# Slot projections: group sums taken by TensorE, and the inverse root spread by a product

## The chip, the cores and the metric

The kernel runs on one core of a Trainium2 chip. The time is device time in microseconds (us), from start to end of one execution. TensorE (PE; its weight loads PEld), VectorE (DVE), ScalarE (ACT) and GpSimd (POOL) each work through a queue of their own; SyncE (SP) issues most DMAs. The profile counts times from the first instruction of one profiled execution.

## The reference, cut to what matters

The input is an image of 512 x 512 positions with 64 channels. Two layers follow each other; the part that concerns us is the beginning of the first.

```python
x = x + _L0_conv_ref(_gn(x), ...)     # the first layer
...
def _ln(x, w, b):
    mu = jnp.mean(x, axis=-1, keepdims=True)
    var = jnp.var(x, axis=-1, keepdims=True)
    return (x - mu) * jax.lax.rsqrt(var + EPS) * w + b
xn = _ln(x, norm_w, norm_b)
left = xn @ left_w + left_b
right = xn @ right_w + right_b
m = sequence_mask.astype(xn.dtype)
mask = (m[:, :, None] * m[:, None, :])[..., None]
left = left * mask
right = right * mask
left = left * jax.nn.sigmoid(xn @ lgate_w + lgate_b)
right = right * jax.nn.sigmoid(xn @ rgate_w + rgate_b)
...
out = jnp.einsum('bkjd,bkid->bijd', left, right)
```

So each position is normalised over its 64 channels, projected to a left and a right side, and each side is multiplied by a gate. Where the mask is zero, left and right are zero; the kernel therefore computes them only for the rows and columns that the mask keeps, the "slots".

## The kernel before

The kernel ranks the positions that the mask keeps. If no more than K = 256 are kept, which holds here, the function `compact` does the work. Its first stage reads the image, takes the statistics for the group norm, and copies the kept columns into one large buffer `xc` in SBUF: 128 partitions (kept rows, in two halves `r`), K + 1 columns, two halves, 64 channels. The second stage, which the change touches, makes the left and right sides from `xc` and stores them to DRAM (`left_d`, `right_d`). Later stages multiply the two sides (`tri_c_ps`), normalise, project, gate, add to the image and do the second layer.

The second stage works on 64 groups `q` of four kept columns each. A group is a tile of 128 x 512 elements. In "channel-major" form its partitions are 64 channels of row half 0 and 64 channels of row half 1, and its 512 elements are four columns by 128 rows. Each group passes through these functions:

- `channels(q)` (L704): four transposes by TensorE (L707) turn four columns of `xc` to channel-major form in PSUM (`xc_ps`); ScalarE applies the group norm's scale and offset (L709) and writes a tile `gc_t` in SBUF.
- `centered(q)` (L713): four matmuls (L716) with the tile as the stationary operand and the constant matrix `center` as the moving one. They subtract the mean over the channels, and turn the tile back: the result `cc_ps` has positions as partitions. ScalarE squares it (L720, `sqc`).
- in the loop, VectorE sums the squares over 64 channels (L778): eight sums for each partition and group (`total`). After four groups (QB = 4) there is a 128 x 32 tile.
- `factors(k)` (L726): nine small VectorE operations (L199 to L209, in `rsqrt_steps`) compute the inverse square root of the 128 x 32 tile. They are kept in a list `todo`, and each iteration of the loop issues the next three.
- `spread(q)` (L730): GpSimd copies the eight factors of a group to 64 channels each (L733, `rbc`, 128 x 512).
- `normed(q)` (L735): four transposes (L739) bring the factors to channel-major form in PSUM (`rc_ps`); VectorE multiplies `gc_t` by them (L741, `xnc`).
- `project(q, k)` (L743): matmuls with 64 rows (L747), one for each row half, for the gates and for the sides, into PSUM tiles of two banks each (`gates_c`, `sides_c`).
- ScalarE takes the sigmoid of the gates (L756, `sigc`); VectorE adds the bias to the sides and multiplies by the sigmoid (L773, two operations, `o_c`); SP issues two stores (L783).

The order is written out by hand: the engines take the operations in the order of the program. A loop runs over `q` from -10 to 63. One iteration issues, in this order: gates and sigmoid of group q; `normed(q + 1)`; up to three root steps; `spread(q + 2)`; `channels(q + 10)`; `centered(q + 9)`; sides and `o_c` of group q; the sums of squares of q + 9; the stores of group q. So ten iterations run ahead before the first gates, and the last ten have nothing left to centre. [...]PSUM banks of 2 KB are in use: two for `xc_ps`, one each for `cc_ps` and `rc_ps`, four for `gates_c` and `sides_c`, which have one buffer each. `sigc` has one buffer too.

A float32 matmul appears in the profile as two instructions, a transpose as one.

Of the kernel before, what the change touches and what calls it, by code (L numbers as in the profile page):

```python
# [9 lines left out]
F32 = mybir.dt.float32  # L10
I32 = mybir.dt.int32
AF = mybir.ActivationFunctionType
ALU = mybir.AluOpType
AX = mybir.AxisListType
PSUM = bass.MemoryType.PSUM
DRAM = bass.MemoryType.DRAM

P = 128
N = 512
C = 64  # L20
# [8 lines left out]
EPS = 1e-5  # L29
# [5 lines left out]
QB = 4  # L35
# [11 lines left out]
def conv_preact_kernel(ctx: ExitStack, tc: tile.TileContext, t: dict):  # L47
    nc = tc.nc
    x, out = t["x"], t["out"]
# [17 lines left out]
    ident = load_const("c_ident", [P, P])  # L67
    center = load_const("c_center", [P, P])
# [13 lines left out]
    with tc.tile_pool(name="ix", bufs=1) as xp, tc.tile_pool(  # L82
        name="ixp", bufs=1, space=PSUM
# [105 lines left out]
            step()  # L189
        return out  # L190

    def rsqrt_steps(pool, total, scale, eps, shape, y=None):

        v, w, h, out = (pool.tile(shape, F32, name="rq_" + k) for k in ("v", "w", "h", "out"))
        if y is None:
            y = pool.tile(shape, F32, name="rq_y")
        vec = nc.vector
        return out, [
            lambda: vec.tensor_scalar(v, total, scale, eps, ALU.mult, ALU.add),  # L199
            lambda: vec.tensor_scalar(y.bitcast(I32), v.bitcast(I32), -0.5, float(0x5F3759DF), ALU.mult, ALU.add),  # L200

            lambda: vec.tensor_mul(w, y, v),
            lambda: vec.tensor_mul(h, w, y),
            lambda: vec.scalar_tensor_tensor(h, h, -10.0 / 3.0, h, ALU.add, ALU.mult),
            lambda: vec.scalar_tensor_tensor(y, h, 5.0, y, ALU.add, ALU.mult),

            lambda: vec.tensor_mul(w, y, v),
            lambda: vec.scalar_tensor_tensor(w, w, -0.5 * 27.0 / 512.0, y, ALU.mult, ALU.mult),
            lambda: vec.scalar_tensor_tensor(out, w, 9.0 / 16.0, y, ALU.add, ALU.mult),  # L209
        ]  # L210
# [402 lines left out]
    def compact(fc):  # L613
# [31 lines left out]
        with tc.tile_pool(name="xc", bufs=1) as cp:  # L645
            xc = cp.tile([P, K + 1, 2, C], F32, name="xc")
            with tc.tile_pool(name="f1", bufs=1) as sp, tc.tile_pool(name="f1x", bufs=2) as xp, tc.tile_pool(
                name="f1y", bufs=4
# [19 lines left out]
                for jc in range(NJ):  # L668
                    if jc % quarter == 0:
                        stats = sp.tile([P, 1, 16 * quarter, 6], F32, name="stats1c")  # L670
                    for r in range(4):
                        flat = xgs[jc][1][r].rearrange("p j c -> p (j c)")
# [18 lines left out]
                ab1 = group_norm_affine(fc, sets, 2 * stats.shape[2], "xc")  # L691


            with tc.tile_pool(name="fb", bufs=QB + 8) as gp, tc.tile_pool(name="fw", bufs=2) as wk, tc.tile_pool(
                name="fr", bufs=3
            ) as rp, tc.tile_pool(name="fg", bufs=1) as sp, tc.tile_pool(name="fo", bufs=2) as op, tc.tile_pool(
                name="fpt", bufs=2, space=PSUM
            ) as pt, tc.tile_pool(name="fpc", bufs=1, space=PSUM) as pc, tc.tile_pool(
                name="fpp", bufs=1, space=PSUM
            ) as pp, tc.manual_schedule():  # L700
                groups = K // 4
                gts, totals, rss, rbs, xns, todo = {}, {}, {}, {}, {}, []

                def channels(q):  # L704
                    tps = pt.tile([P, 4, P], F32, name="xc_ps")
                    for i in range(4):
                        nc.tensor.transpose(tps[:, i, :], xc[:, 4 * q + i].rearrange("p r c -> p (r c)"), ident)  # L707
                    gts[q] = gp.tile([P, N], F32, name="gc_t")
                    nc.scalar.activation(  # L709
                        gts[q], tps.rearrange("p i k -> p (i k)"), AF.Identity, bias=ab1[:, 1:2], scale=ab1[:, 0:1]  # L710
                    )

                def centered(q):  # L713
                    cps = pc.tile([P, 8, C], F32, name="cc_ps")
                    for i in range(4):
                        nc.tensor.matmul(  # L716
                            cps[:, 2 * i : 2 * i + 2, :], gts[q][:, i * P : (i + 1) * P], center, start=True, stop=True
                        )
                    sq = wk.tile([P, 8, C], F32, name="sqc")
                    nc.scalar.activation(sq, cps, AF.Square)  # L720
                    k, n = divmod(q, QB)
                    if n == 0:
                        totals[k] = rp.tile([P, QB * 8], F32, name="total")
                    return sq, totals[k][:, 8 * n : 8 * n + 8]

                def factors(k):  # L726
                    rss[k], steps = rsqrt_steps(rp, totals.pop(k), 1.0 / C, EPS, [P, QB * 8])
                    todo.extend(steps)

                def spread(q):  # L730
                    k, n = divmod(q, QB)
                    rbs[q] = rp.tile([P, 8, C], F32, name="rbc")
                    nc.gpsimd.tensor_copy(rbs[q], rss[k][:, 8 * n : 8 * n + 8].unsqueeze(2).to_broadcast([P, 8, C]))  # L733

                def normed(q):  # L735
                    rps = pc.tile([P, N], F32, name="rc_ps")
                    flat = rbs.pop(q).rearrange("p (i r) c -> p i (r c)", r=2)
                    for i in range(4):
                        nc.tensor.transpose(rps[:, i * P : (i + 1) * P], flat[:, i, :], ident)  # L739
                    xns[q] = wk.tile([P, N], F32, name="xnc")  # L740
                    nc.vector.tensor_mul(xns[q], gts.pop(q), rps)  # L741

                def project(q, k):  # L743
                    ps = pp.tile([P, 2, N], F32, name=k + "_c")
                    for r in range(2):
                        h = slice(r * C, (r + 1) * C)
                        nc.tensor.matmul(ps[:, r, :], weights[k][h], xns[q][h], start=True, stop=True)  # L747
                    return ps


                for q in range(-QB - 6, groups):
                    live = lambda i: 0 <= q + i < groups
                    if live(0):
                        gates = project(q, "gates")
                        sig = sp.tile([P, 2, N], F32, name="sigc")
                        nc.scalar.activation(sig, gates, AF.Sigmoid, bias=biases["gates"])  # L756
                    if live(1):
                        normed(q + 1)
                    for step in todo[:3]:
                        step()  # L760
                    del todo[:3]
                    if live(2):
                        spread(q + 2)
                    if live(QB + 6):
                        channels(q + QB + 6)
                    if live(QB + 5):
                        sq, total = centered(q + QB + 5)
                    if live(0):
                        sides = project(q, "sides")
                        xns.pop(q)  # L770
                        res = op.tile([P, 4, 2, P], F32, name="o_c")
                        for r in range(2):
                            nc.vector.scalar_tensor_tensor(  # L773
                                res[:, :, r, :], sides[:, r].rearrange("p (i k) -> p i k", i=4), biases["sides"],
                                sig[:, r].rearrange("p (i k) -> p i k", i=4), ALU.add, ALU.mult,
                            )
                    if live(QB + 5):
                        nc.vector.tensor_reduce(total, sq, AX.X, ALU.add)  # L778
                        if (q + QB + 5) % QB == QB - 1:
                            factors((q + QB + 5) // QB)  # L780
                    if live(0):
                        for side, dst in enumerate((left_d, right_d)):
                            nc.sync.dma_start(  # L783
                                dst[:, 4 * q : 4 * q + 4, :].rearrange("c j k -> c (j k)"),
                                res[side * C : (side + 1) * C].rearrange("c j r k -> c (j r k)"),
                            )
# [20 lines left out]
        with tc.tile_pool(name="tri", bufs=1) as trp:  # L807
# [17 lines left out]
            with tc.tile_pool(name="ti", bufs=4) as ip, tc.tile_pool(name="tt", bufs=3) as tp, tc.tile_pool(  # L825
                name="tpt", bufs=4, space=PSUM
            ) as ps_t, tc.tile_pool(name="tpo", bufs=3, space=PSUM) as ps_o:
                for c in range(C):
                    sides = []
                    for name, src in (("left", left_d), ("right", right_d)):  # L830
                        raw = ip.tile([P, 2, K], F32, name=name + "_raw")
                        nc.sync.dma_start(raw, src[c].rearrange("(b p) k -> p b k", p=P))
                        tps = ps_t.tile([P, 2, K], F32, name="side_ps")
# [31 lines left out]
            with tc.manual_schedule(), tc.tile_pool(name="late", bufs=1) as lp:  # L865
# [65 lines left out]
                with tc.tile_pool(name="np_x", bufs=LEAD + 2) as tp, tc.tile_pool(  # L931
                    name="np_y", bufs=2
                ) as yp, tc.tile_pool(name="np_q", bufs=2) as sqp, tc.tile_pool(
                    name="np_s", bufs=3
                ) as small, tc.tile_pool(name="oz", bufs=4) as zp, tc.tile_pool(
                    name="o1", bufs=1
# [15 lines left out]
                    totals = [scratch[:, i, : SIZE * 8] for i in range(2)]  # L952

                    factors = [scratch[:, i, SIZE * 8 :] for i in range(2)]
                    eps = lp.tile([P, 1], F32, name="eps")
# [420 lines left out]
def _constants():  # L1376
# [19 lines left out]
    for part, rows_ in enumerate(((c.T, -s.T), (s.T, c.T))):  # L1396
# [6 lines left out]
        "c_last_mask": last_mask,  # L1403
        "c_pick4": (np.arange(P) % 32 % MODES % 4)[:, None] == np.arange(4)[None, :],
        "c_col_inv": col_inv.reshape(P, 2, 4, P),
        "c_turn": np.kron([[0, 1], [-1, 0]], np.eye(C)),
        "c_iota": np.tile(np.arange(N), (P, 1)),
        "c_tri": np.triu(np.ones((P, P))),
# [33 lines left out]
```

## Time and profile before

| | |
|---|---|
| median of three runs | 1838.84 us (1837.78 to 1840.75) |
| profiled execution | 1839.54 us, its span 1837.7 us |
| mean granted TensorE clock | 0.894 |
| slot projections | from about 206 to 466 us of the span |
| stores of the sides | 64 of 256 KB for each side |

Operations of the stage, each with its count and median duration in ns:

| operation | engine | count | ns |
|---|---|---|---|
| `gc_t`, 128x512 from PSUM | ACT | 64 | 770 |
| `sqc`, 128x512 from PSUM | ACT | 64 | 595 |
| `sigc`, 128x1024 from PSUM | ACT | 64 | 1114 |
| `total`, 128x512 to 128x8 | DVE | 64 | 677 |
| root steps, 128x32 | DVE | 9 x 16 | 174 to 193 |
| `xnc`, 128x512 | DVE | 64 | 679 |
| `o_c`, 128x512 | DVE | 128 | 746 |
| `rbc`, 128x512 | POOL | 64 | 613 |

How to read what follows: the timeline lists start, duration, engine, line, operation and tile, with a count where like instructions are merged. A matmul's duration runs until its end, and the next one starts before that, so the cost of a piece of TensorE's work is read from start to start. The list of waits gives the total in us, the times, and the longest.

### The profile page before, as it was taken

Reading aid. Unit: us, or ns where it says so; the run is one execution under the profiler, and the core shown is the slowest. Engines: PE = TensorE matmul, PEld = TensorE weight load, DVE = VectorE, ACT = ScalarE, POOL = GpSimd, SP = SyncE. Lnnn points to the kernel's source line nnn. Section 1 sums busy time; section 2 is a strip of 40 time slices with the busy share of each in tenths; the row PEclk is TensorE's granted clock in tenths of the full one; section 3 lists DMA queues with packets and bytes.
Section 4 is the critical chain, followed back from the end, with each engine's and each line's share of the span. In section 5 each row is a group of like instructions: output and inputs, shape, how many; then the busy total and the mean of one; then the engine's idle time right before and its main releaser. Section 6 shows DMA issues by size and latency. Waiting matters only on the chain.

```text
span 1837.7 us, 33577 instructions
## 1 busy us (share of the span) xinstructions
PE 1637.7 (89%) x11414; PEld 1287.7 (70%) x11414; DVE 1423.6 (77%) x2973; ACT 961.9 (52%) x1708; POOL 945.3 (51%) x711
## 2 busy tenths in 40 slices
PE   6779799999799999999999999999999866998772
PEld 5667666665678878897788888888888744665441
DVE  5989777777455547788999999999999975675552
ACT  3555555555222259976777777777777631111000
POOL 3666211111000006788999999999999862211110
PEclk9989899999899999999999999999999966555555
DMA  6999255556656513667777876776777698999999
GB/s 255 381 375 371 106 127 138 138 138 154 208 174 182 177 41 141 224 234 257 254 244 249 279 269 233 241 274 234 253 258 258 210 273 338 411 426 426 427 427 379
DMA packets 188453, 467.94 MB, mean 255 GB/s; under 512 B 34672, under 2 KB 134000, under 8 KB 147184
## 3 DMA queue, kind: packets, MB, share of 16 engines
q1 hardware_dynamic: 157376, 262.21, 42.5%
q0 software_dynamic: 27712, 201.40, 29.1%
q10 hardware_dynamic: 3184, 2.08, 0.4%
q8 instruction: 93, 1.52, 0.3%
q14 instruction: 88, 0.72, 0.1%
HBM read 278.05 MB, written 187.56 MB: 253 GB/s over the span
## 4 chain that ended last, share of the span: by engine, by line
PE 29%; DVE 16%; DMA 9%; POOL 4%; issue 3%; ACT 1%; DVEq 0%; POOLq 0%; ACTq 0%
PE c_ps L979 6%; PE w_ps L979 6%; PE t_ps L969 5%; PE l_ps L1348 4%; DVE stats2c L1097 4%; DMA places<-x_h,dst_i 4%; PE y_ps L990 4%; DVE z_t L1195 3%; DVE scratch L1012 3%; DVE z_t L1201 3%; PE f_ps L1069 2%; POOL z_t L1038 2%; DMA out_x<-places 2%; POOL places L1042 2%; DMA lx_t<-x_h,dst_i 2%
## 5 line engine op out<-in xcount | busy, mean ns | idle before, releaser
L979 PE MATMUL w_ps<-gate_x,xt_c 128*128 128x128 f32 x2048 | 280.1, 280 | 32.1 <-DVE z_t L1195 26.7
L1042 POOL TENSOR_TENSOR places<-places,z_t 128x1024 f32<-128x1024 f32 x127 | 301.2, 2371 | 8.0
L979 PEld LDWEIGHTS w_ps<-gate_x,xt_c 128*128 128x128 f32 x2048 | 251.5, 194 | 47.8 <-DVE z_t L1195 43.4
L979 PE MATMUL c_ps<-center_x,xt_c 128*128 128x128 f32 x2048 | 276.2, 278 | 1.2 <-ACT xt_c L1008 0.6
L979 PEld LDWEIGHTS c_ps<-center_x,xt_c 128*128 128x128 f32 x2048 | 252.1, 194 | 3.9 <-ACT xt_c L974 2.3
L1348 PE MATMUL l_ps<-places,rinv 24*128 24x512 f32 x512 | 207.8, 1124 | 29.3 <-DVE places L1355 18.6
L1097 DVE BATCH_NORM_STATS2 stats2c<-places 128x6 f32<-128x128 f32 x1024 | 220.5, 278 | 12.5 <-POOL places L1042 12.5
L1012 DVE TENSOR_REDUCE scratch<-sq_c 128x16 f32<-128x1024 f32 x160 | 194.6, 1216 | 27.9 <-ACT sq_c L1007 18.7
L1146 ACT ACTIVATE z_t<-z_t 128x1024 f32<-128x1024 f32 x128 | 135.5, 1059 | 133.7 <-DVE z_t L1201 116.0
L1199 POOL TENSOR_TENSOR z_t<-z_t,bias_row_out 128x1024 f32<-128x1024 f32 x32 | 75.7, 2365 | 246.6 <-DVE z_t L1195 242.5
L969 PE MATMUL t_ps<-c_ident,places 128*128 128x128 f32 x1280 | 199.0, 278 | 1.3 <-DVE places L854 1.3
L1348 PEld LDWEIGHTS l_ps<-places,rinv 24*128 24x128 f32 x512 | 120.3, 303 | 111.9 <-DVE places L1355 59.6
L969 PEld LDWEIGHTS t_ps<-c_ident,places 128*128 128x128 f32 x1280 | 144.5, 142 | 60.6 <-issue 50.3
L974 ACT ACTIVATE xt_c<-t_ps,ab_xc 128x512 f32<-128x512 f32 x256 | 176.0, 687 | 10.7 <-PE t_ps L969 9.8
L1195 DVE TENSOR_TENSOR z_t<-w_ps,rs_n 128x512 f32<-128x512 f32 x256 | 171.9, 672 | 3.7 <-PE w_ps L979 3.5
L1004 ACT ACTIVATE sq_c<-c_ps 128x512 f32<-128x512 f32 x256 | 150.5, 588 | 30.9 <-PE c_ps L979 29.4
L679 DVE BATCH_NORM_STATS2 stats1c<-x_ps 128x6 f32<-128x512 f32 x256 | 155.6, 681 | 12.5 <-PE x_ps L678 12.2
L1201 DVE TENSOR_TENSOR z_t<-z_t,scratch 128x1024 f32<-128x1024 f32 x128 | 156.3, 1221 | 10.0 <-ACT rs_n L1018 3.8
L1038 POOL TENSOR_TENSOR z_t<-z_t,places 128x1024 f32<-128x1024 f32 x64 | 151.6, 2369 | 16.2 <-ACT z_t L1146 13.3
L1355 DVE TENSOR_TENSOR places<-places,l_ps 128x512 f32<-128x512 f32 x176 | 110.2, 683 | 56.1 <-DMA places<-x_h,dst_i 45.5
L1038 POOL TENSOR_TENSOR z_t<-z_t,bias_row_out 128x1024 f32<-128x1024 f32 x63 | 149.4, 2371 | 4.6 <-ACT z_t L1146 4.0
L733 POOL COPY rbc<-rq_out 128x512 f32<-128x512 f32 x64 | 38.3, 613 | 210.0 <-DVE rq_out L209 132.0
(212 smaller groups left out, 2748.8 us busy)
## 6 DMA issues: line engine op xcount, KB each, us to landing
x_h<-places SPq DMA_DIRECT2D x64, 1024.0 KB
out_x<-places SPq DMA_DIRECT2D x44, 1024.0 KB
places<-u_d SPq DMA_DIRECT2D x512, 64.0 KB
out_x<-lx_t SPq DMA_DIRECT2D x20, 1024.0 KB
left_d<-o_c SPq DMA_DIRECT2D x64, 256.0 KB
right_d<-o_c SPq DMA_DIRECT2D x64, 256.0 KB
left_raw<-left_d SPq DMA_DIRECT2D x64, 256.0 KB
right_raw<-right_d SPq DMA_DIRECT2D x64, 256.0 KB
```

The costliest lines, as they stand in the source:

```text
L679: nc.vector.bn_stats(stats[:, 0, 16 * (jc % quarter) + 4 * r + c, :], ps.rearrange("p i k -> p (i k)"))
L969: nc.tensor.transpose(tps[:, i, :], flat[:, o : o + P], ident)
L974: nc.scalar.activation(xts[s], tps, AF.Identity, bias=ab1[:, 2:3])
L979: nc.tensor.matmul(ps[:, 2 * i : 2 * i + 2, :], xts[s][:, i, :], w, start=True, stop=True)
L1004: nc.scalar.activation(sq, cps, AF.Square)
L1012: nc.vector.tensor_reduce(totals[k % 2][:, 8 * (n - 1) : 8 * (n + 1)], sqs.pop(s // 2), AX.X, ALU.add)
L1038: nc.gpsimd.tensor_mul(zs[k, c], zs[k, c], u)
L1042: nc.gpsimd.tensor_add(xr, xr, zs.pop((k, c)))
L1097: nc.vector.bn_stats(st[k // 4][:, g, k % 4, :], x_of(k)[:, :, 2 * g : 2 * g + 2])
L1195: nc.vector.tensor_mul(z[:, 8 * odd : 8 * odd + 8, :], wps, rs)
L1201: nc.vector.tensor_add(z, z, bias_ps["ogate"].unsqueeze(1).to_broadcast([P, 16, C]))
L1348: nc.tensor.matmul(ps.rearrange("p j o -> p (j o)"), rinv[h, b, :], it[h], start=True, stop=True, tile_position=(32 * g, 0),)
```

## The change

The squares stay channel-major, and TensorE sums them. `centered` makes one matmul with `center` stationary and the whole tile of 512 positions moving. A new function `summed` takes four groups at once: for each, a matmul with a 128 x 32 matrix of zeros and ones (`sum_w`) sums the squares over the 64 channels of each row half. The four write to four strips of 32 partitions of one PSUM tile `total_ps` (column tiles, `tile_position`); a second set of four groups is added to the same tile, on other partitions. So the tile holds a row for each of eight groups and two halves, 16 rows of 512 that matter, the rest being zero. The root steps then run once for eight groups, on 128 x 512 elements, two in an iteration. `normed` spreads the factors by one matmul with another matrix of zeros and ones (`row_w`) in place of GpSimd's copy and four transposes. The channel-major group is written back into `xc`, in place of a tile of its own. `xc_ps` has one buffer. The loop runs 16 iterations ahead where it ran 10. Two constants (128 KB and 512 KB) are loaded at the start of the stage by SP.

```diff
-    def rsqrt_steps(pool, total, scale, eps, shape, y=None):
+    def rsqrt_steps(pool, total, scale, eps, shape, y=None, out=None):
...
-            with tc.tile_pool(name="fb", bufs=QB + 8) as gp, tc.tile_pool(name="fw", bufs=2) as wk, tc.tile_pool(
-                name="fr", bufs=3
+            with tc.tile_pool(name="fs", bufs=6) as qp, tc.tile_pool(name="fw", bufs=2) as wk, tc.tile_pool(
+                name="fr", bufs=1
...
-                name="fpt", bufs=2, space=PSUM
+                name="fpt", bufs=1, space=PSUM
...
+                sum_w = sp.tile([P, 8, 32], F32, name="sum_wc")
+                nc.sync.dma_start(sum_w, t["c_sum_w"])
+                row_w = sp.tile([P, 2 * QB, P], F32, name="row_w")
+                nc.sync.dma_start(row_w, t["c_row_w"])
+                def gts(q):
+                    return xc[:, 4 * q : 4 * q + 4].rearrange("p i r c -> p (i r c)")
...
                 def centered(q):
-                    cps = pc.tile([P, 8, C], F32, name="cc_ps")
-                    for i in range(4):
+                    cps = pc.tile([P, N], F32, name="cc_ps")
+                    nc.tensor.matmul(cps, center, gts(q), start=True, stop=True)
+                    sqs[q] = qp.tile([P, N], F32, name="sqc")
+                    nc.scalar.activation(sqs[q], cps, AF.Square)
+                def summed(q):
+                    k, a = divmod(q // QB, 2)
+                    if a == 0:
+                        totals[k] = pc.tile([P, N], F32, name="total_ps")
+                    for g in range(QB):
                         nc.tensor.matmul(
-                            cps[:, 2 * i : 2 * i + 2, :], gts[q][:, i * P : (i + 1) * P], center, start=True, stop=True
+                            totals[k][32 * g : 32 * g + 32, :], sum_w[:, a, :], sqs.pop(q + g),
+                            start=(a == 0), stop=(a == 1), tile_position=(0, 32 * g),
                         )
...
                 def factors(k):
-                    rss[k], steps = rsqrt_steps(rp, totals.pop(k), 1.0 / C, EPS, [P, QB * 8])
+                    out = rp.tile([P, N], F32, name="factors", bufs=2)
+                    rss[k], steps = rsqrt_steps(rp, totals.pop(k), 1.0 / C, EPS, [P, N], out=out)
                     todo.extend(steps)
-                def spread(q):
-                    k, n = divmod(q, QB)
-                    rbs[q] = rp.tile([P, 8, C], F32, name="rbc")
-                    nc.gpsimd.tensor_copy(rbs[q], rss[k][:, 8 * n : 8 * n + 8].unsqueeze(2).to_broadcast([P, 8, C]))
                 def normed(q):
                     rps = pc.tile([P, N], F32, name="rc_ps")
-                    flat = rbs.pop(q).rearrange("p (i r) c -> p i (r c)", r=2)
-                    for i in range(4):
-                        nc.tensor.transpose(rps[:, i * P : (i + 1) * P], flat[:, i, :], ident)
+                    k, n = divmod(q, 2 * QB)
+                    nc.tensor.matmul(rps, row_w[:, n, :], rss[k], start=True, stop=True)
                     xns[q] = wk.tile([P, N], F32, name="xnc")
-                    nc.vector.tensor_mul(xns[q], gts.pop(q), rps)
+                    nc.vector.tensor_mul(xns[q], gts(q), rps)
...
-                for q in range(-QB - 6, groups):
+                ahead = 15
+                for q in range(-ahead - 1, groups):
...
-                    for step in todo[:3]:
+                    for step in todo[:2]:
                         step()
-                    del todo[:3]
-                    if live(2):
-                        spread(q + 2)
-                    if live(QB + 6):
-                        channels(q + QB + 6)
-                    if live(QB + 5):
-                        sq, total = centered(q + QB + 5)
+                    del todo[:2]
+                    if live(ahead + 1):
+                        channels(q + ahead + 1)
+                    if live(ahead):
+                        centered(q + ahead)
+                    done = q + ahead - QB
+                    if live(ahead - 1) and done % QB == 0:
+                        summed(done)
+                        if done % (2 * QB) == QB:
+                            factors(done // (2 * QB))
...
-                    if live(QB + 5):
-                        nc.vector.tensor_reduce(total, sq, AX.X, ALU.add)
-                        if (q + QB + 5) % QB == QB - 1:
-                            factors((q + QB + 5) // QB)
```

More of the change, by code (lines that the diff above doesn't have):

```diff
@@ L190, in rsqrt @@
         return out
-    def rsqrt_steps(pool, total, scale, eps, shape, y=None):
-        v, w, h, out = (pool.tile(shape, F32, name="rq_" + k) for k in ("v", "w", "h", "out"))
+    def rsqrt_steps(pool, total, scale, eps, shape, y=None, out=None):
+        v, w, h = (pool.tile(shape, F32, name="rq_" + k) for k in ("v", "w", "h"))
+        if out is None:
+            out = pool.tile(shape, F32, name="rq_out")
         if y is None:
@@ L701, in compact @@
                 groups = K // 4
-                gts, totals, rss, rbs, xns, todo = {}, {}, {}, {}, {}, []
+                sqs, totals, rss, xns, todo = {}, {}, {}, {}, []
+                sum_w = sp.tile([P, 8, 32], F32, name="sum_wc")
[4 more added lines that the diff above has]
+                    return xc[:, 4 * q : 4 * q + 4].rearrange("p i r c -> p (i r c)")
                 def channels(q):
@@ L707, in channels @@
                         nc.tensor.transpose(tps[:, i, :], xc[:, 4 * q + i].rearrange("p r c -> p (r c)"), ident)
-                    gts[q] = gp.tile([P, N], F32, name="gc_t")
                     nc.scalar.activation(
-                        gts[q], tps.rearrange("p i k -> p (i k)"), AF.Identity, bias=ab1[:, 1:2], scale=ab1[:, 0:1]
+                        gts(q), tps.rearrange("p i k -> p (i k)"), AF.Identity, bias=ab1[:, 1:2], scale=ab1[:, 0:1]
                     )
                 def centered(q):
-                    cps = pc.tile([P, 8, C], F32, name="cc_ps")
@@ L716, in centered @@
                         nc.tensor.matmul(
-                            cps[:, 2 * i : 2 * i + 2, :], gts[q][:, i * P : (i + 1) * P], center, start=True, stop=True
-                        )
-                    sq = wk.tile([P, 8, C], F32, name="sqc")
-                    nc.scalar.activation(sq, cps, AF.Square)
-                    k, n = divmod(q, QB)
-                    if n == 0:
-                        totals[k] = rp.tile([P, QB * 8], F32, name="total")
-                    return sq, totals[k][:, 8 * n : 8 * n + 8]
+                            totals[k][32 * g : 32 * g + 32, :], sum_w[:, a, :], sqs.pop(q + g),
@@ L726, in factors @@
+                            start=(a == 0), stop=(a == 1), tile_position=(0, 32 * g),
+                        )
                 def factors(k):
-                    rss[k], steps = rsqrt_steps(rp, totals.pop(k), 1.0 / C, EPS, [P, QB * 8])
+                    out = rp.tile([P, N], F32, name="factors", bufs=2)
+                    rss[k], steps = rsqrt_steps(rp, totals.pop(k), 1.0 / C, EPS, [P, N], out=out)
                     todo.extend(steps)
-                def spread(q):
-                    k, n = divmod(q, QB)
-                    rbs[q] = rp.tile([P, 8, C], F32, name="rbc")
-                    nc.gpsimd.tensor_copy(rbs[q], rss[k][:, 8 * n : 8 * n + 8].unsqueeze(2).to_broadcast([P, 8, C]))
@@ L1405, in _constants @@
         "c_col_inv": col_inv.reshape(P, 2, 4, P),
+        "c_sum_w": np.arange(32)[None, None, :] == 2 * np.arange(8)[None, :, None] + half[:, None, None],
+        "c_row_w": np.arange(P)[:, None, None]
+        == (32 * (np.arange(8) % 4) + 2 * (np.arange(8) // 4))[None, :, None] + half[None, None, :],
         "c_turn": np.kron([[0, 1], [-1, 0]], np.eye(C)),
```

## The prediction

> **What bounds the kernel now.** The edit touches one stage, the slot projections, so I read the busy times in three windows first: its head (groups are centred, none projected yet), its middle, and its tail (nothing left to centre).
>
> ```profile
> core 0: us, PE busy (x) PEld busy (x) DVE busy (x) ACT busy (x) POOL busy (x), PEclk, DMA share, GB/s
> 209.70:227.60 17.90, 16.50 (x108) 14.61 (x108) 7.63 (x19) 11.18 (x18) 2.34 (x4) 0.85 0.00 0
> 227.60:434.00 206.40, 206.38 (x1294) 133.97 (x1296) 158.78 (x339) 123.31 (x163) 31.15 (x52) 1.00 0.53 134
> 434.00:465.70 31.70, 28.78 (x128) 11.19 (x126) 24.31 (x45) 12.58 (x13) 4.79 (x8) 1.00 0.71 175
> ```
>
> In the middle TensorE is busy 206.38 of 206.40 us at the full granted clock; VectorE has 159 us of work, ScalarE 123, GpSimd 31. Since ends of matmuls are modelled, busy alone proves little, so the next view is the timeline of TensorE over one period:
>
> ```profile
> 301.51 0.66 PE L739 MATMUL rc_ps<-c_ident,rbc 128*128 128x128 f32 x4
> ...
> 302.01 0.60 PE L707 MATMUL xc_ps<-c_ident,xc 128*128 128x128 f32 x4
> ...
> 302.44 1.06 PE L716 MATMUL cc_ps<-c_center,gc_t 128*128 128x128 f32 x8
> ...
> 303.43 1.13 PE L747 MATMUL sides_c<-xnc,w_sides 64*128 64x512 f32 x4
> ...
> 304.39 1.02 PE L747 MATMUL gates_c<-xnc,w_gates 64*128 64x512 f32 x4
> ...
> 305.35 0.66 PE L739 MATMUL rc_ps<-c_ident,rbc 128*128 128x128 f32 x4
> ```
>
> From start to start: spread transposes 0.50, transposes to channels 0.43, centring 0.99, sides 0.96, gates 0.96; a period is 3.84 us. No piece has a gap in front of it. The list of waits for the stage says the same: no matmul waits long for anybody, while the others wait for the loop.
>
> ```profile
> PE cc_ps L716 <- ACT sqc L720: 1.3, 5, 0.3
> PEld rc_ps L739 <- POOL rbc L733: 11.4, 15, 0.8
> DVE o_c L773 <- ACT sqc L720: 43.5, 54, 1.3
> ```
>
> The second line is a weight load that comes late under a running matmul, not a stop of TensorE. The third is VectorE with time to spare. So VectorE's `total` reductions (64 of 677 ns) and GpSimd's `rbc` copies (64 of 613 ns), which the change removes, lie beside TensorE's work and buy nothing in the middle; what counts there is TensorE's own sum.
>
> The tail has another limit:
>
> ```profile
> 447.30 1.41 DVE L773 SCALAR_TENSOR_TENSOR o_c<-sides_c,b_sides,sigc 128x512 f32<-128x512 f32 x2
> ...
> 448.85 1.13 PE L747 MATMUL sides_c<-xnc,w_sides 64*128 64x512 f32 x4
> ...
> 449.99 1.13 PE L747 MATMUL gates_c<-xnc,w_gates 64*128 64x512 f32 x4
> 450.08 1.41 DVE L773 SCALAR_TENSOR_TENSOR o_c<-sides_c,b_sides,sigc 128x512 f32<-128x512 f32 x2 [0.64 <-PE sides_c L747]
> ```
>
> One `sides_c` buffer: the matmuls wait until the previous `o_c` has read it, 1.13 + 1.41 plus two hand-overs, 2.78 at least; the ten last groups took 2.93 each. In the head one `cc_ps` buffer ties centring to `sqc`: cc starts at 217.08, 218.93, 220.77, a period of 1.85 us (1.16 matmuls, 0.60 square, hand-overs).
>
> **Prices from other stages.** The stage has no full-height 512-column product and no column-tiled one. Two other stages have their like, at granted clock 1.00:
>
> ```profile
> 529.72 1.99 PE L850 MATMUL tri_c_ps<-left_t,right_t 128*128 128x256 f32 x8
> 531.55 0.49 PE L836 MATMUL side_ps<-c_ident,right_raw 128*128 128x128 f32 x3
> ...
> 1015.68 1.06 PE L979 MATMUL c_ps<-center_x,xt_c 128*128 128x128 f32 x8
> 1016.66 1.06 PE L1069 MATMUL f_ps<-places,hb 128*32 128x512 f32 x8
> 1017.66 0.66 PE L969 MATMUL t_ps<-c_ident,places 128*128 128x128 f32 x4
> ```
>
> Eight instructions (four products, two each) of 256 columns take 1.83 us, so one product of 256 columns is 0.458 and one of 512 columns about 0.88 (twice 0.427 of streaming, plus some 15 ns an instruction). Four column-tiled products of 512 columns take 1.00 us together, not four times 0.88.
>
> **What the Trainium skill says.** "FP8 and Floating Point Precision", section "TensorE Precision Notes": true float32 takes four passes through the array. The trace agrees: 0.458 us for 256 columns is 4.3 cycles of 2.4 GHz a column, in two instructions. A transpose is one instruction and takes 0.43/4 = 0.108 us for 128 columns, half of a product. This is the heart of the forecast: a spread by transposes becomes a spread by products. "TensorEngine Tiling (Array Packing)", section "Key Properties": tiles run in parallel, and a change of tiling mode drains TensorE. Agrees: the four tiles of `f_ps` overlap, and centring costs 0.99 before the half-height `sides` but 0.89 elsewhere (1008.12 to 1009.01 for `w_ps`), a drain of about 0.1.
>
> **The change, part by part**, in TensorE time per group in the middle:
> 1. Centring: eight 128-column instructions become two of 512. 0.88 plus the same drain of 0.1 before `sides`: 0.98 against 0.99, -0.01. At best (no instruction overhead, a smaller drain) -0.15; at worst 0.
> 2. Sums: four column-tiled products every fourth iteration, 1.00 plus some 0.06 for the extra change of mode: 1.06/4 = +0.265. Lower end 0.21 (streaming alone); upper end 0.53, if each tile's second instruction holds up the next tile.
> 3. Spread: four transposes (0.43 and 0.07 drain after `gates`) become one 512-column product, 0.88 + 0.07 = 0.95: +0.45; from +0.37 to +0.45.
> 4. Transposes to channels, gates and sides: unchanged. The period becomes 3.84 + 0.70 = 4.54 us; I use 4.52, since the pieces' overheads above are rounded up; from 4.27 to 4.85.
>
> VectorE loses 0.677 + 9 x 0.187/4 = 1.10 us a group, and gains nine root steps of 128x512 every eight groups. No such step is on view; binary operations of 512 elements are 0.68 (`xnc`) to 0.75 (`o_c`), one-source ones 0.48 (`hot`), so I take 0.65 each, 0.73 a group. Its load falls from about 3.3 to 2.9 of 4.5 us. Two steps (1.3) in an iteration make 1.3 + 0.68 + 1.41 = 3.4, hidden in the middle, not in the tail. GpSimd has nothing left here. ScalarE's three operations (0.770, 0.595, 1.114) stay; `gc_t` now lands in `xc` itself, over columns whose transposes have already been read.
>
> One bank for `xc_ps` where there were two: the next transposes wait for `gc_t`. In the middle they start at 305.84 while `gc_t` ended at 304.14; in the head `gc_t` ends at 217.70, transposes start at 217.97. No cost. The sums add a wait of TensorE for `sqc` of the iteration before, with `sides` queued behind: that square ended at 304.62, and a sum comes after the centring that starts at 306.28. The ninth root step falls one iteration ahead of the first spread that reads it. Both hidden, by 1.7 us and by about half an iteration.
>
> Two loads on SP at the stage's start, 128 and 512 KB: SP issues nothing between the stage's begin and 233.33, and DMA moves nothing from about 202 to 231. At the some 400 GB/s that this core's DMA reached just before 202, 640 KB is some 2 us; the first use is the first sum, around 218. Hidden; without that cover about 2 us once. Nothing is queued behind them before the first store.
>
> **The sum by phase.** Head: six more iterations before the first gates, each bound by the centring-square loop. That loop is 1.04 (matmuls to their end) + 0.60 + 0.09 = 1.73. Six of them 10.4; nine older iterations 0.1 shorter, -0.9; three sums, each 1.06 with some 0.43 of slack between centring and square, +1.9. First gates move from 227.6 to 239.0 (+11.4). Middle: 48 iterations instead of 54: 48 x 4.52 = 217.0 against 54 x 3.83 = 206.8. Tail: 16 groups instead of 10. TensorE then has 0.96 + 0.95 + 0.95 = 2.86, just over the `sides_c` loop; five of them carry root steps and are VectorE's at 3.4: 16 x 2.87 + 2.5 = 48.4 against 29.3. Together +11.4 + 10.2 + 19.1 = +40.7 us.
>
> The profiled execution took 1839.54 us with a span of 1837.7; with the change 1880.2. The median of the runs is 0.7 lower, 1838.84, so I say 1879. No later stage changes: it starts when the last `o_c` is stored, 40 us later.
>
> **Rivals.**
> A. The sum above: 1879, between 1860 and 1900 by the bounds (low: 4.27 in the middle, 48 x 4.27 = 205.0, head +9, tail 45, +23; high: 4.85, head +13, tail 53, +63, ends not all met at once). Chance 0.80.
> B. Column tiles do not overlap here, because consecutive instructions of one tile block the next: a sum costs 4 x 0.88 = 3.5, 0.88 a group, 0.61 more over 60 groups, +37: 1916. For: each product is two instructions. Against: `f_ps` has the same form and took 1.00. 0.07.
> C. Writing back into `xc` ties all readers of that buffer to its newest write: centring of the older group would wait for `gc_t` of the new one, 0.77 plus hand-over, about 0.9 over 48 iterations, +43: 1922. For: it is one tile. Against: `places` is one tile too, and there transposes run while other parts are filled (TensorE busy 12.00 of 12.00 us from 1008 to 1020). 0.06.
> D. Not slower: long products stream faster than their short likes, because what the 128- and 256-column products show is the cost of loading weights, which now happens a quarter as often. With 0.44 for 512 columns, spread stays at 0.50, centring falls to 0.54, sums to 0.15: period 3.53, 48 x 3.53 = 169.4, head +5, tail 47.3, -14: 1825. It decides from about 0.56 us a product downwards: there the period is 3.82, and 48 x 3.82 + 47.3 plus a head 5 longer equal the old 206.8 + 29.3. For: weight loads of 0.19 us stand beside every short product. Against: loads in centring come every 0.12 us while the 256-column products take 0.23 an instruction, so they stream, and are not held by loads. 0.07.
>
> Runs tell 0.2% apart (3.7 us). A to C are slower; D is mostly faster, some of it within. Faster 0.05, the same 0.02, slower 0.93. Range 1860 to 1900.
>
> **What would show it.** TensorE still without gaps in the middle at a period near 4.5; spread and centring each at 0.88 to 1.0 from start to start, sums about 1.05 every fourth time; first gates near 239; VectorE and GpSimd idler with no gain. Wrong: a 512-column product near 0.44, gaps before centring (C), sums of 2 us or more (B), or a middle that TensorE does not fill, which would mean that I took the wrong bound.

## The result, and the profile after

The changed kernel takes 1881.15 us (median of four runs, 1878.89 to 1884.21) against 1838.31 us before (four runs, one more than in the table above): a ratio of 1.0244, with a 95% interval from 1.0224 to 1.0265. That is 43 us more. The profiled execution has a span of 1882.3 us against 1837.7.

First the page of the changed kernel, its lines of busy time and instructions:

```profile
PE 1681.9 (89%) x11030; PEld 1241.8 (66%) x11030; DVE 1410.5 (75%) x2837; ACT 963.1 (51%) x1708; POOL 906.8 (48%) x647
```

The change did what it was written to do: 384 matmul instructions and 136 VectorE instructions fewer, GpSimd 38 us less busy, VectorE 13. Yet TensorE is 44 us busier (1637.7 before), and the kernel is longer by the same amount. Fewer matmuls, more matmul time: a count of instructions says nothing as long as their columns are not counted.

Where it happened is read from the busy time by window, with the windows cut at the changed kernel's own phases: head, middle (first gates to the gates of group 48) and tail.

```profile
core 0: us, PE busy (x) PEld busy (x) DVE busy (x) ACT busy (x) POOL busy (x), PEclk, DMA share, GB/s
209.70:240.20 30.50, 28.89 (x114) 12.74 (x112) 6.65 (x10) 19.31 (x29) 0.00 (x0) 0.92 0.00 1
240.20:457.30 217.10, 217.10 (x867) 86.31 (x868) 132.25 (x196) 110.89 (x147) 0.00 (x0) 1.00 0.45 113
457.30:510.50 53.20, 50.94 (x170) 15.06 (x166) 38.93 (x58) 18.41 (x17) 0.00 (x0) 1.00 0.62 157
```

TensorE fills the middle as before, at the full clock. VectorE's share there has fallen from 77% (158.78 of 206.40) to 61%, weight loads from 65% to 40%, GpSimd's to zero, and the kernel gained nothing by it. From the stage's first transposes to the first matmul behind the stage it is 205.8 to 511.2, or 305.4 us, against 206.5 to 466.0, or 259.5, before. The stage is 45.9 us longer. What lies before it took 206.5 us and now 205.8, what follows 1371.7 and now about 1371: the rest of the kernel has only moved.

The timeline of TensorE over one iteration, here one with a set of sums (column one is the start, column two the duration):

```profile
335.96 1.12 PE L747 MATMUL rc_ps<-factors,row_w 128*128 128x512 f32 x2
...
336.92 0.60 PE L717 MATMUL xc_ps<-c_ident,xc 128*128 128x128 f32 x4
...
337.36 1.02 PE L724 MATMUL cc_ps<-xc,c_center 128*128 128x512 f32 x2
...
338.31 1.07 PE L734 MATMUL total_ps<-sqc,sum_wc 128*32 128x512 f32 x8
...
339.31 1.13 PE L755 MATMUL sides_c<-xnc,w_sides 64*128 64x512 f32 x4
...
340.27 1.02 PE L755 MATMUL gates_c<-xnc,w_gates 64*128 64x512 f32 x4
...
341.22 1.13 PE L747 MATMUL rc_ps<-factors,row_w 128*128 128x512 f32 x2
```

From start to start: spread 0.96 (it was 0.50), transposes 0.44, centring 0.95 (0.99), sums 1.00, sides 0.96, gates 0.95. An iteration takes 5.26 us with sums and 4.27 without, 4.52 in the mean, against 3.84. Two instructions of 512 columns in the spread take about twice the time of four transposes of 128.

The list of waits for the stage shows the other side. TensorE waits for nobody for long, and the others wait for it:

```profile
PE xc_ps L717 <- ACT xc L718: 2.0, 1, 2.0
...
PE cc_ps L724 <- ACT sqc L726: 1.5, 6, 0.3
...
DVE o_c L785 <- PE sides_c L755: 62.7, 52, 3.1
DVE xnc L749 <- PE rc_ps L747: 31.9, 61, 3.8
```

Before, VectorE's largest wait in front of `o_c` was 43.5 us; now it waits 62.7 us for the sides and 31.9 us for the spread factors. Time was taken off VectorE and given to TensorE, in a stage that TensorE bounds.

### The profile page after: what moved, and what is told of

It is laid out like the page before. It is cut to its first block, busy times and chain, and to the rows that moved or that the text cites. A ratio compares the mean times of both kernels' runs of the same rounds, so it can differ in the third digit from the quotient of the medians.

```text
span 1882.3 us, 32491 instructions
## 1 busy us (share of the span) xinstructions
PE 1681.9 (89%) x11030; PEld 1241.8 (66%) x11030; DVE 1410.5 (75%) x2837; ACT 963.1 (51%) x1708; POOL 906.8 (48%) x647
## 4 chain that ended last, share of the span: by engine, by line
PE 52%; DVE 20%; DMA 13%; issue 5%; POOL 4%; ACT 3%; SPq 1%; POOLq 1%; ACTq 0%; DVEq 0%
DMA out_x<-places 8%; PE tri_c_ps L858 7%; PE w_ps L987 6%; PE c_ps L987 5%; PE t_ps L977 4%; DVE stats2c L1105 4%; PE y_ps L998 4%; DVE scratch L1020 4%; DVE z_t L1203 4%; PE rc_ps L747 3%; PE sides_c L755 3%; PE cc_ps L724 3%; DVE stats1c L681 3%; DVE z_t L1209 3%; PE l_ps L1356 3%
## 5 line engine op out<-in xcount | busy, mean ns | idle before, releaser
L987 PE MATMUL w_ps<-gate_x,xt_c 128*128 128x128 f32 x2048 | 281.3, 281 | 31.9 <-DVE z_t L1203 28.4
```

Source lines behind the costliest of these rows:

```text
L987: nc.tensor.matmul(ps[:, 2 * i : 2 * i + 2, :], xts[s][:, i, :], w, start=True, stop=True)
```

## The experiments

The theory: the stage lasts as long as TensorE streams columns, so each piece is worth its streamed time, and the work taken off VectorE and GpSimd is worth nothing. The rivals: waits between the engines hold the stage; the sums hide; long products are cheaper than short ones because they load weights more rarely; something on VectorE was on the path after all. Each run is compared with runs of the kernel before on the same chip, whose median was 1836.7 us for the first four, 1833.5 for the next two and 1834.4 for the last.

### The spread in half the streaming time

```diff
-nc.tensor.matmul(rps, row_w[:, n, :], rss[k], start=True, stop=True)
+for j, part in enumerate(rss[k]):          # high and low part, bfloat16
+    nc.tensor.matmul(rps, row_h[:, n, :], part, start=(j == 0), stop=(j == 1))
...
+todo.append(lambda: nc.vector.tensor_copy(hi, out))
+todo.append(lambda: nc.vector.tensor_sub(lo, out, hi))
...
-ahead = 15
+ahead = 16
```

> The spread by one float32 product becomes two bfloat16 products (high and low part of the factor, added in PSUM), which halves its streaming and keeps the factor to some 16 bits. TensorE-bound theory: a spread falls from 0.96 to about 0.52 us from start to start, 47 middle iterations gain 0.44 each (-21), the tail falls to the sides loop (-3), the extra iteration of lead costs +1: about 1858 us, 20 above the kernel before. Rival, that the stage is held by waits between engines and not by TensorE's streaming: 1878 or more.

Measured: 1856.03 us, ratio to before 1.0100 (1.0079 to 1.0121). The timeline of TensorE:

```profile
322.18 0.39 PE L755 MATMUL rc_ps<-factors_hi,row_h 128*128 128x512 bf16 x1
322.41 0.38 PE L755 MATMUL rc_ps<-factors_lo,row_h 128*128 128x512 bf16 x1
322.62 0.60 PE L720 MATMUL xc_ps<-c_ident,xc 128*128 128x128 f32 x4
```

The spread takes 0.44 us in place of 0.96 and the mean iteration 4.00 in place of 4.52, although VectorE got two more operations every eight groups. The loss against before is 1.0% in place of 2.4%. The rival, by which waits hold the stage and the run would gain nothing, is out: the spread is more than half of the loss.

### The sums in a quarter of the streaming time

```diff
+sum_h = sp.tile([P, 8, 32], BF16, name="sum_h")
+nc.vector.tensor_copy(sum_h, sum_w)
...
-sqs[q] = qp.tile([P, N], F32, name="sqc")
+sqs[q] = qp.tile([P, N], BF16, name="sqc")
...
-totals[k][32 * g : 32 * g + 32, :], sum_w[:, a, :], sqs.pop(q + g),
+totals[k][32 * g : 32 * g + 32, :], sum_h[:, a, :], sqs.pop(q + g),
```

> The squares and the matrix of the sums are bfloat16, so a set of four column-tiled sums streams a quarter of the cycles; the squares are rounded to 8 bits, which changes the result a little. TensorE-bound theory: a set falls from 0.99 to about 0.30 us, 16 sets gain 0.69 each: about 1870 us. Rival, that the sums hide in the gaps of other work: 1881, no change.

Measured: 1869.63 us, ratio 1.0182 (1.0162 to 1.0202). The timeline of TensorE around a set of sums:

```profile
314.59 1.02 PE L727 MATMUL cc_ps<-xc,c_center 128*128 128x512 f32 x2
315.55 0.40 PE L737 MATMUL total_ps<-sqc,sum_h 128*32 128x512 bf16 x4
315.88 1.13 PE L758 MATMUL sides_c<-xnc,w_sides 64*128 64x512 f32 x4
```

A set takes 0.33 us in place of 1.00, and the kernel follows. So the sums lie on the path with their full time.

### The long product cut into short ones

```diff
-nc.tensor.matmul(cps, center, gts(q), start=True, stop=True)
+for i in range(4):
+    part = slice(i * P, (i + 1) * P)
+    nc.tensor.matmul(cps[:, part], center, gts(q)[:, part], start=True, stop=True)
```

> Centring of the changed kernel in four products of 128 columns in place of one of 512, with the same result. If streaming sets the price: 8 x 0.111 = 0.89 plus the drain, within 0.03 us of the long product, so 1881 to 1883 us. Rival, that a long product is cheaper because it loads weights a quarter as often: 0.1 us or more a group, 1888 us or more.

Measured: 1883.23 us, ratio 1.0255 (1.0233 to 1.0278), against 1.0244 (1.0224 to 1.0265) for the changed kernel. In the trace centring takes 0.98 us from start to start in place of 0.95, at the same number of columns and four times the weight loads. The loads hide almost wholly under the matmuls; the columns are the price.

### The kernel before, without the work that the change takes away

```diff
-nc.gpsimd.tensor_copy(rbs[q], rss[k][:, 8 * n : 8 * n + 8].unsqueeze(2).to_broadcast([P, 8, C]))
+rbs[q] = rb_all                            # constant ones
...
-nc.vector.tensor_reduce(total, sq, AX.X, ALU.add)
-factors((q + QB + 5) // QB)
```

> The kernel before, with VectorE's sums over channels, the root steps and GpSimd's copies of the factors left out (constant factors of one are spread instead, so left and right are not normalised). It shows what removing that work is worth by itself. TensorE-bound theory: nothing in the middle, at most 2 us in all from late copies: 1836 to 1839 us. Rival, that this work was on the path: 1825 us or less.

Measured: 1833.83 us, ratio 0.9988 (0.9977 to 0.9999): by the ratio 2.2 us less, with an interval from 0.2 to 4.2, of some 109 us of VectorE and GpSimd work in the stage (64 x 0.677 + 144 x 0.187 + 64 x 0.613). The timeline of TensorE shows the same period as before, 3.84 us:

```profile
300.33 1.02 PE L748 MATMUL gates_c<-xnc,w_gates 64*128 64x512 f32 x4
...
304.17 1.02 PE L748 MATMUL gates_c<-xnc,w_gates 64*128 64x512 f32 x4
```

That is what the removed work was worth. The change paid 43 us for about 2.

### Without the centring product

The mean can be had without a product that centres: from sums of the values and of the squares.

```diff
-cps = pc.tile([P, N], F32, name="cc_ps")
-nc.tensor.matmul(cps, center, gts(q), start=True, stop=True)
 sqs[q] = qp.tile([P, N], F32, name="sqc")
-nc.scalar.activation(sqs[q], cps, AF.Square)
+nc.scalar.activation(sqs[q], gts(q), AF.Square)
...
+for j in range(2):
+    for g in range(QB):
+        nc.tensor.matmul(
+            totals[k][j][32 * g : 32 * g + 32, :], sum_w[:, a, :],
+            sqs.pop(q + g) if j else gts(q + g), ...
...
+nc.scalar.activation(m, first, AF.Square, scale=1.0 / C)
+nc.vector.scalar_tensor_tensor(var, second, 1.0 / C, m, ALU.mult, ALU.subtract)
...
-ahead = 15
+ahead = 16
```

> The centring product is left out: the squares are taken of the channel-major group itself, TensorE sums both the values and the squares (two sets of column-tiled products), and the variance is the mean square less the squared mean. TensorE-bound theory: 0.95 less for centring and 0.25 more for the second sums, 0.70 a group over 47 middle iterations, -33, +1 for one more iteration of lead: about 1848 us. Rival, that with TensorE's work at 3.82 us a group another loop takes over (ScalarE's chain through the one bank of the transposes, or VectorE): 1860 us or more.

Measured: 1848.75 us, ratio 1.0085 (1.0066 to 1.0104). The timeline of TensorE around the sums:

```profile
317.05 1.06 PE L733 MATMUL total_ps<-xc,sum_wc 128*32 128x512 f32 x8
317.93 1.04 PE L733 MATMUL total_ps<-sqc,sum_wc 128*32 128x512 f32 x8
318.90 1.13 PE L761 MATMUL sides_c<-xnc,w_sides 64*128 64x512 f32 x4
```

Two sets take 1.85 us. The mean iteration is 3.88 us, close to the 3.82 that the columns give, and no other loop took over.

### Both, and then their order

The run without the centring product, with the spread in two bfloat16 products whose parts GpSimd makes (lead 17):

> As the run without the centring product, and the spread in two bfloat16 products, with the high and low part made by GpSimd. TensorE-bound theory: 0.96 + 0.96 + 0.44 + 0.52 + 0.50 = 3.38 us a group against 3.84 before; with the longer lead about 1822 us, 0.8% under the kernel before. Rival, that VectorE (0.69 + 1.41 + two root steps of 0.68 = 3.46 us in seven of eight iterations) or ScalarE takes over as the bound: 1830 to 1840 us.

Measured: 1830.04 us, ratio 0.9985 (0.9975 to 0.9995). The first theory gave 1822, the rival 1830 to 1840, whose lower end it meets. Its middle takes 3.58 us an iteration (gates from 268.83 to 383.35, 32 iterations; the 3.64 in the next expectation is too high), where TensorE's pieces add up to less than 3.4, and now TensorE has gaps: it is busy 159.89 of 163.30 us from 240.7 to 404. The timeline of ScalarE and VectorE in the iteration behind a set of sums:

```profile
329.14 0.59 ACT L746 ACTIVATE moment_m<-total_ps 128x512 f32<-128x512 f32 x1
...
329.62 0.78 ACT L721 ACTIVATE xc<-xc_ps,ab_xc 128x512 f32<-128x512 f32 x1
329.76 0.69 DVE L748 SCALAR_TENSOR_TENSOR moment_v<-total_ps,moment_m 128x512 f32<-128x512 f32 x1 [1.16 <-ACT moment_m L746]
...
330.37 1.40 DVE L799 SCALAR_TENSOR_TENSOR o_c<-sides_c,b_sides,sigc 128x512 f32<-128x512 f32 x2
...
331.92 1.13 PE L769 MATMUL sides_c<-xnc,w_sides 64*128 64x512 f32 x4 [0.52 <-DVE o_c L799]
```

VectorE stood 1.16 us for ScalarE's square of the first moment, which came behind the sigmoid; `o_c`, queued behind the root step, was late, and the sides waited 0.52 us for their one buffer. This happens once in eight groups: such an iteration takes 3.76 us, its neighbours 2.99. The last run changes the order, on ScalarE and on VectorE at once:

```diff
-todo.append(lambda: nc.scalar.activation(m, first, AF.Square, scale=1.0 / C))
+nc.scalar.activation(m, first, AF.Square, scale=1.0 / C)    # right behind the sums
...
-for step in todo[:2]:
-    step()
-del todo[:2]
+if todo:
+    todo.pop(0)()
...                                        # o_c of this iteration
+if todo:
+    todo.pop(0)()
...
-ahead = 17
+ahead = 16
```

> As the run without the centring product and with the split spread, but ScalarE squares the first moment right behind the sums, and of the two root steps of an iteration one comes behind the gated sides on VectorE; the lead is one iteration shorter. In the run before this one the middle took 3.64 us a group where TensorE's work is 3.38. If the order on VectorE and ScalarE made the difference: 3.4 us a group over 48 iterations, -9, and -2 from the lead: about 1820 us. If the wait is elsewhere: 1828 to 1830 us.

Measured: 1828.05 us, ratio 0.9962 (0.9948 to 0.9977); its runs scatter from 1819.6 to 1830.9, more than the others'. Its profiled execution (1821.72 us) is one of three short ones, up to 1821.7; the others lie from 1825.8 up. The windows of its head, middle and tail:

```profile
203.60:236.00 32.40, 20.40 (x118) 10.27 (x117) 9.92 (x26) 20.72 (x32) 1.77 (x2) 0.78 0.04 14
236.00:400.00 164.00, 163.99 (x853) 64.32 (x854) 125.14 (x200) 112.83 (x149) 10.63 (x12) 1.00 0.58 145
400.00:452.00 52.00, 48.08 (x184) 12.88 (x182) 41.05 (x65) 20.94 (x21) 1.77 (x2) 1.00 0.71 179
```

In the middle TensorE has no gaps again (busy 163.99 of 164.00, and no matmul of it waits), at 3.47 us an iteration (gates from 254.81 to 338.12, 24 iterations). That is 0.11 less than in the run before, and the iterations of 3.76 us are gone, which were worth some 0.1 a group: the order was the cause of this part. Which of the two orders did it was not separated. Some 0.09 us over TensorE's own 3.38 remains; weight loads of the gates wait for the sigmoid there, 35 times and 24.2 us between 240 and 400.

The forecast of 1820 holds for these three of eleven executions; the median falls where the other forecast, a wait elsewhere, had put it. So the timeline shows what the order did in one execution, and the whole kernel shows less of it. Of the 17.8 us by which the profiled span (1819.9) lies below that of the kernel before, the stage gives 10.9 (248.6 in place of 259.5, first transposes to first matmul behind the stage); the rest lies outside the code that was changed. Why most executions are longer was not pursued; those of 1828 us and more show a mean granted clock of 0.888 to 0.891, the three short ones 0.893 to 0.894, and whether that is cause or effect is open. By the ratios the version beats both kernels, by 0.4% and 2.7%. What it still gives away is the head: 32 us, in which TensorE works 20; in most of its iterations the transposes wait 0.87 us for ScalarE to empty the one buffer of `xc_ps`.

## Why the prediction was right

Said: 1879 us, slower; measured: 1881.15. The mechanism was right. That the number fits within 2 us is in part luck: in the profiled execution the stage is 45.9 us longer and the sum said 40.7, the head and the tail both having been put too short; but this execution is the longest of the four, 3 us over their median. The steps against the trace:

**The bound.** TensorE's streaming, not the work of VectorE and GpSimd. Shown from both sides: taking that work away is worth 2 us (`before_less`), halving the spread's or quartering the sums' streaming gives 25 and 12 us (1881.15 less 1856.03 and 1869.63; from the ratios with the same sign and size). The prices from the timeline agree with the whole: 64 spreads of 0.46 more, 16 sets of 1.00 and 64 centrings of 0.04 less make 43 of the 45.9 us. The longer lead was not run by itself; by this sum it costs a few us at most.

**Prices in the middle.** Spread 0.95 said, 0.96 measured; centring 0.98 and 0.95; a set of sums 1.06 and 1.00; iteration 4.52 and 4.52. The prices came from other stages, those of spread and centring from products of another shape, and carried over since columns and tiling mode were alike. The sum of the parts was 4.54; that 4.52 was written for it was a rounding that happened to fit. Middle: 217.0 said, 217.06 measured (240.23 to 457.29).

**The head** came out longer, by 13.3 us where 11.4 was said (first transposes to first gates: 34.45 against 21.11). Three terms were too small. The loop of centring and square takes 1.81 us, not 1.73, as the end of the second long product comes 1.12 after its start and not 1.04; this makes some 0.9 us over the head. The one bank for `xc_ps`, put at no cost, costs once at the start: the transposes of the second group wait 2.0 us for ScalarE (the list of waits above), and the first centring begins 4.0 us behind the first transposes, where it was 3.2. And the first spread falls into the head, with some 0.4 us that nothing hides. The sums' share was right: centring starts at 218.81 and 221.36, 0.74 more than without a set.

**The tail** is the largest miss: +22.6 us (53.88 against 31.25, from the gates of the first tail group to the first matmul behind the stage) where +19.1 was said. One part of it was left out. The last ten iterations of the kernel before, and the last sixteen of the changed one, were taken to have nothing left to centre; the first of them still centres the last group. The second holds the last set of sums, which the forecast charged to no phase. The profile of the changed kernel:

```profile
457.29 1.02 PE L755 MATMUL gates_c<-xnc,w_gates 64*128 64x512 f32 x4
...
459.20 1.02 PE L724 MATMUL cc_ps<-xc,c_center 128*128 128x512 f32 x2
...
461.12 1.02 PE L755 MATMUL gates_c<-xnc,w_gates 64*128 64x512 f32 x4
...
463.13 1.06 PE L734 MATMUL total_ps<-sqc,sum_wc 128*32 128x512 f32 x8
...
465.09 1.02 PE L755 MATMUL gates_c<-xnc,w_gates 64*128 64x512 f32 x4
```

These two iterations take 3.83 and 3.97 us where 2.87 was put: 2.1 us. The other part is the price of a plain group, further on in the tail:

```profile
486.89 1.13 PE L755 MATMUL sides_c<-xnc,w_sides 64*128 64x512 f32 x4
...
487.81 0.33 PEld L755 LDWEIGHTS gates_c<-xnc,w_gates 64*128 64x128 f32 x4 [0.61 <-ACT sigc L765]
487.86 1.11 PE L755 MATMUL gates_c<-xnc,w_gates 64*128 64x512 f32 x4
...
488.90 1.12 PE L747 MATMUL rc_ps<-factors,row_w 128*128 128x512 f32 x2
...
489.95 1.13 PE L755 MATMUL sides_c<-xnc,w_sides 64*128 64x512 f32 x4
```

A group takes 3.06 us, not 2.86; over the nine groups without root steps this makes 1.9 us. The spread takes 1.05 here, since it stands between two half-height products and pays a change of tiling mode at both ends; 0.95 counted one, as in the middle, where transposes follow. Where it stands between full-height products, in the head, it takes 0.86:

```profile
237.98 1.02 PE L747 MATMUL rc_ps<-factors,row_w 128*128 128x512 f32 x2
238.84 0.60 PE L717 MATMUL xc_ps<-c_ident,xc 128*128 128x128 f32 x4
```

The tail of the kernel before could have told it: its four transposes of a spread take 0.60 there, and 0.50 in the middle.

```profile
445.26 0.66 PE L739 MATMUL rc_ps<-c_ident,rbc 128*128 128x128 f32 x4
445.86 1.13 PE L747 MATMUL sides_c<-xnc,w_sides 64*128 64x512 f32 x4
```

The gates take 1.04, not 0.95: their weight loads wait for the sigmoid to free `gates_c`, a wait that the forecast put at nothing. The groups with root steps took 3.3 to 3.5 us, as said, but four of them and not five came out longer.

**Covers.** The loads of the two constants were hidden (issued at 201.17 and 201.56, moved by 205 us at 200 to 250 GB/s and not 400, first used at 219.87). Root steps of 128x512 measured 0.68 us for two sources and from PSUM, 0.43 for one source in SBUF, where 0.65 was taken for all. VectorE hides them in the middle. Its load there was put at 3.3 us a group before and 2.9 after, from durations; the windows give 2.95 (158.78 us over 53.8 periods) and 2.76, since the operations overlap a little.

**Rivals.** B (tiles one after the other, 3.5 us a set) is refuted by 1.00; C (the write into `xc` holds centring back) by the lack of any such wait in the list; D (long products cheaper) by the spread at 0.96 and by the run with short products.

The Trainium skill's two statements: four passes for float32, in "FP8 and Floating Point Precision", section "TensorE Precision Notes", agree with the runs, as two bfloat16 products of 512 columns took 0.44 us together, and one float32 product 0.86, about four times one of them. The drain on a change of tiling mode, in "TensorEngine Tiling (Array Packing)", section "Key Properties", agrees with the spread's 0.86, 0.96 and 1.05 us at none, one and two changes; it was used where it stood in the trace of before and missed where the new order made one more. Ahead of the bfloat16 spread no such cost was seen.

## What to carry to other kernels

Before work is moved onto an engine, ask whether that engine fills the stage, and price the new work there in its own unit: columns times passes for TensorE, not instructions. A float32 product used as a transpose or a broadcast pays twice what a transpose of the same columns pays; where the matrix is zeros and ones, the moving side split in two bfloat16 parts halves that, at a little less precision. When a product is put between others, count the changes of tiling mode at both of its ends, in every phase of the loop.

## What the hardware showed that was not expected

- Two bfloat16 products of 512 columns on the spread's path take 0.44 us from start to start with the mode change included, less than the 0.52 expected: the second starts 0.23 after the first, and the transposes 0.21 after that. The 0.07 us of drain counted ahead of the spread was not seen there.
- The first root step, the same one-source operation on 128x512 elements, takes 0.68 us on a tile in PSUM (changed kernel) and 0.42 on one in SBUF (`moments_split`); two sources in SBUF take 0.68 as well. So where the operand lies matters as much as the number of sources.

```profile
467.81 0.68 DVE L201 TENSOR_SCALAR rq_v<-total_ps 128x512 f32<-128x512 f32 x1
...
332.28 0.42 DVE L202 TENSOR_SCALAR rq_v<-moment_v 128x512 f32<-128x512 f32 x1
```

- Two sets of column-tiled sums in a row start 0.88 us apart (317.05 to 317.93) where a set between other products takes 1.00, and the second of the two 0.97: about 0.1 us of a set goes with the change of mode behind it.
